# Two graph-attention layers on one core: edge places held as bytes, and layer 2 builds its edge masks instead of loading the stored ones

## The chip, the core and the metric

The kernel runs on one core of a Trainium2 chip. The metric is the device time of one launch in microseconds (us). The engines are PE (TensorE; its weight loads are listed apart as PEld), DVE (VectorE), ACT (ScalarE), POOL (GpSimd) and SP (SyncE), which only issues transfers here. [...]

## What is computed

The input is 6250 nodes with 768 numbers each and 100,000 directed edges, sorted by the node they end at. Each node is also given an edge to itself. Cut to what matters, the reference is:

```python
h = maximum(layernorm(x), 0)
for W, a_src, a_dst, heads in layers:        # 4 heads, then 1; 256 features
    h = h @ W
    e = leaky_relu(alpha_s[src] + alpha_d[dst], 0.2)    # alpha = sums of h * a
    alpha = softmax of e over the edges with the same dst
    h = relu(segment_sum(h[src] * alpha, dst) + bias)
out = x + (relu(h @ Wm1 + bm1) @ Wm2 + bm2)
```

Every edge needs a row of its source node (a gather), a number of its target node (found through a mask), and has to be added up at its target node (a product with a one-hot matrix).

## The kernel before, in words

**Phase 1** (lines 301 to 459) normalises x, multiplies it by W1 and stores 49 blocks of 128 rows as `table[1]`. Beside it a generator, `edge_places` (line 189), turns the target indices into places within a block of 128. It makes two forms. `dcol` (line 126) has one place per edge for each lane, in f32. `dmod_d` (line 127) is a DRAM copy of all places in a row, in bf16; they are made in `drm` (line 206) and stored at line 214. Padding edges have a bit far above 127 set, so that they match no lane.

**Layers.** `layer_edges` (line 525) is run for layer 1 and for layer 2. The edges are cut into tiles of 128 edges, four tiles are a group g, and four groups are a block t of 128 target nodes. There are NG = 196 groups and NT = 49 blocks, so 782 real tiles per layer. The loop at line 705 goes over g, with j = g % 4:

- `gather(g + 8)` (line 551, POOL) fetches the rows of four tiles, eight groups ahead. There are ten buffers G.
- `pair(g, 0)` and `pair(g, 1)` (line 611) each treat two tiles: two exponentials on ACT (lines 619, 621), short products on DVE (lines 624, 627 or 634), then the weighted operand `hw` on DVE (line 636 in layer 1, two instructions at line 631 in layer 2), then two products on PE (line 647) that add up in `o_ps`.
- `make_hot(g + 1)` (line 581, DVE) builds the one-hot operand, in layer 1 only.
- at j = 0: `fetch_rows(t + 4)` (line 513), which loads the places of 16 tiles, spread to all 128 lanes, into a `drow` buffer (three of them, shared with other uses), again in layer 1 only; `node.prefetch(t)`, which in layer 2 loads x; and `meet(t + 1)` (line 591), 16 small bf16 products of the masks with a table `win`, which give each edge its target's number.
- at j = 1 and j = 3: `make_mask((g + 7) // 2)`.
- `gather_up(g - 2)` (line 658): DVE adds `o_ps` of two groups back into a running sum (`acc`, line 672), and ACT copies a quarter of it (line 680).
- `advance(g)` steps the work of finished blocks: `Node1.steps` (line 794) or `Node2.steps` (line 900), with transposes and products on PE, copies on ACT (`rT`, line 767) and, in layer 2, the output store on SP (line 946).

A mask covers eight tiles: 128 lanes by 1024 edges in bf16, one where the edge's place equals the lane. This is the function around the change:

```python
            def make_mask(u):
...
                if layer == 2:
                    return fetch_mask(u + 1)
                a, b = (t * P for t in both(u))
                mask[u] = maskp.tile([P, 8 * P], BF16, name="mask")
...
                nc.vector.tensor_scalar(mask[u][:, a:b], drow[u // 2][:, at + a:at + b], pidx, None,
                                        ALU.is_equal)
                nc.sync.dma_start(mask_d[u * P:(u + 1) * P], mask[u])
```

So layer 1 makes each of its 98 masks on DVE (line 570) and stores it to DRAM (`mask_d`, line 299, stored at 572). Layer 2 loads the same masks back (line 523). Both layers use the same six mask buffers in turn. Five loads are issued at the end of layer 1 (line 753).

**The order of the work is written out by hand** (`manual_schedule`, line 300): each engine gets its instructions in the order of the Python program, and waits are put in where data or buffers demand them. SP's queue holds, in that order, the loads of places, masks and x, and the stores of masks, table rows and outputs; a store that waits for its data holds up what stands behind it.

Between the layers, `first_rows`, `first_hits` and `first_whole` (lines 288, 249, 262) let the first tiles of a layer start before the last blocks of its table are stored. `first_hits` compares source indices, as 32-bit integers kept in a `drow` buffer, with node numbers (line 258, DVE). `hold` (line 848) checks the limits of the method in block 3 of layer 2 and uses three `drow` buffers for it. If its flag is set, `general` runs at the end; with these inputs it isn't.

Of the kernel before, what the change touches and what calls it, by code (L numbers as in the profile page):

```python
# [10 lines left out]
F32 = mybir.dt.float32  # L11
BF16 = mybir.dt.bfloat16
I32 = mybir.dt.int32
AF = mybir.ActivationFunctionType
ALU = mybir.AluOpType
AX = mybir.AxisListType

P = 128
# [15 lines left out]
NET = NG * TPG  # L34
FIRST = LEAD // P
LAST = -(-(LEAD + E) // P)
NU = NG // 2
# [5 lines left out]
CH = P * TPC  # L43
NCH = EP // CH
# [9 lines left out]
def kernel(  # L54
# [21 lines left out]
    nc = tc.nc  # L76
# [7 lines left out]
    dram = pool("dram", 1, space=bass.MemoryType.DRAM)  # L84
# [38 lines left out]

    src_i = const.tile([P, NET], I32, name="src_i")
    dst_f = const.tile([P, NET], F32, name="dst_f")
    dcol = const.tile([P, NET], F32, name="dcol")
    dmod_d = dram.tile([NCH, CH], BF16, name="dmod_d")
    flags = const.tile([P, 4], F32, name="flags")


# [58 lines left out]
    def edge_places(ones):  # L189

        dst_i = ones.tile([P, NET], I32, name="dst_i")
        dri = ones.tile([NCH, CH], I32, name="dri")
        for to, of in ((dst_i, dst_cols), (dri, dst_rows), (src_i, src_cols)):
            nc.sync.dma_start(to, of)
            yield
            yield
        for layer in bT:
            with nc.allow_non_contiguous_dma(reason="256 numbers"):
                nc.sync.dma_start(bT[layer], {1: b1, 2: b2}[layer].rearrange("(k p) -> p k", p=P))
            yield  # L200
        b = ones.tile([P, OUT_DIM // P], F32, name="b")
        with nc.allow_non_contiguous_dma(reason="768 numbers"):
            nc.sync.dma_start(b, bm2.rearrange("(p k) -> p k", p=P))
        yield

        drm = ones.tile([NCH, CH], BF16, name="drm")
        nc.scalar.activation(dst_f, dst_i, AF.Copy)
        yield
        for d, to in ((dst_i, dcol), (dri, drm)):
            nc.vector.tensor_scalar(d, d, PAD_DST | P - 1, None, ALU.bitwise_and)  # L210
            yield
            nc.scalar.activation(to, d, AF.Copy)
            yield
        nc.sync.dma_start(dmod_d, drm)
        bp = ones.tile([P, 3, OUT_DIM // P], BF16, name="bp")
        rest = ones.tile([P, 2, OUT_DIM // P], F32, name="brest")
        in_parts(nc.vector, [bp[:, k] for k in range(3)], b, rest[:, 0], rest[:, 1])
        yield
        with nc.allow_non_contiguous_dma(reason="768 numbers"):
            nc.sync.dma_start(bm2_d.rearrange("s (p k) -> p s k", p=P), bp)  # L220
# [5 lines left out]
    rowsp = edges_stack.enter_context(tc.tile_pool(name="rows", bufs=3))  # L226
    maskp = edges_stack.enter_context(tc.tile_pool(name="masks", bufs=6))
# [11 lines left out]
    def first_sources(layer):  # L239

        n = len(THERE[layer])
        sources[layer] = []
        for j in range(0, n, 8):
            m = min(n - j, 8)
            of = rowsp.tile([P, 16 * P], BF16, name="drow").bitcast(I32)
            nc.sync.dma_start(of[:, :m * P], bcast(src_rows, m * P, (FIRST + j) * P))
            sources[layer].append(of)

# [39 lines left out]
    def first_rows(layer, stage):  # L288
# [3 lines left out]
        for j in range(j, j + n):  # L292
            g, t = divmod(FIRST + j, TPG)
            if g not in first_G[layer]:
# [1 line left out]
            nc.gpsimd.indirect_dma_start(  # L296
                out=first_G[layer][g][:, t], out_offset=None, in_=table[layer][:there * P],
                in_offset=bass.IndirectOffsetOnAxis(ap=first_i[layer][:, j:j + 1], axis=0))
    mask_d = dram.tile([NU * P, 8 * P], BF16, name="mask_d")
    edges_stack.enter_context(tc.manual_schedule())  # L300
    with tc.tile_pool(name="w1p", bufs=1) as wp, tc.tile_pool(name="x1", bufs=6) as xp, \
            tc.tile_pool(name="wk1", bufs=3) as wk, tc.tile_pool(name="once", bufs=1) as ones:
# [200 lines left out]
    drow, mask = {}, {}  # L503
# [9 lines left out]
    def fetch_rows(r):  # L513

        if r < NET // 16:
            drow[r] = rowsp.tile([P, 16 * P], BF16, name="drow")
            nc.sync.dma_start(drow[r], bcast(dmod_d, 16 * P, r * 16 * P))

    def fetch_mask(u):

        if u < NU:
            mask[u] = maskp.tile([P, 8 * P], BF16, name="mask")
            nc.sync.dma_start(mask[u], mask_d[u * P:(u + 1) * P])

    def layer_edges(layer, H, node, pre, matched, pre_pool):

# [3 lines left out]
        with tc.tile_pool(name=f"eg{layer}", bufs=4) as eg, \  # L530
# [28 lines left out]
            def make_mask(u):  # L559

                if not 0 <= u < NU:
                    return
                if layer == 2:
                    return fetch_mask(u + 1)
                a, b = (t * P for t in both(u))
                mask[u] = maskp.tile([P, 8 * P], BF16, name="mask")
                if u == 0:
                    nc.vector.memset(mask[u][:, :a], 0.0)
                at = u % 2 * 8 * P
                nc.vector.tensor_scalar(mask[u][:, a:b], drow[u // 2][:, at + a:at + b], pidx, None,  # L570
                                        ALU.is_equal)
                nc.sync.dma_start(mask_d[u * P:(u + 1) * P], mask[u])

            def make_hot(g):

# [108 lines left out]
            def advance(g):  # L684

                for _ in range(2 if NG - 4 <= g < NG - 2 else 1):
                    for step in list(late):
                        if next(step, 0) == 0:
                            late.remove(step)

            if layer == 1:
                for r in range(4):
                    fetch_rows(r)
                first_whole(pre_pool, layer)
                for u in range(4):
                    make_mask(u)
            make_hot(0)
            for g in range(AHEAD):
                gather(g)
# [5 lines left out]
            for g in range(NG):  # L705
                t, j = divmod(g, 4)
                if g == NG - 2:
                    at_end.append(g)
                gather(g + AHEAD)
                pair(g, 0)  # L710
                if g == NG - 1:
                    pair(g, 1)
                if g >= NG - 2:
                    gather_up(g - 1)
                advance(g)
                if g <= NG - 4:
                    make_hot(g + 1)
                if g in (NG - 4, NG - 3):
                    make_hot(g + 2)
                if j == 0:  # L720
                    if layer == 1:
                        fetch_rows(t + 4)
                    node.prefetch(t)
                    meet(t + 1)
                elif j == (2 if t < NT - 1 else 1):
                    node.ahead(t)
                elif j % 2:
                    make_mask((g + 7) // 2)
                if g == NG - 3:
                    idle_ps.append(ps.tile([P, 4 * P], F32, name="idle_ps", tag="e"))  # L730
                if g >= NG - 3:
                    stay_warm(3)
                if g < NG - 1:
                    pair(g, 1)
                advance(g)
                if j == 3:
                    join(t + 1)
                if g < NG - 2:
                    gather_up(g - 2)
                if g == NG - 3:  # L740
                    gather_up(g - 1)
                if NG - 3 <= g < NG - 1:
                    stay_warm(3)
                G.pop(g)
                hot.pop(g, None)
                if layer == 1 and g == NG - 6:
                    first_sources(2)
# [1 line left out]
            advance(NG)  # L749
            stay_warm(4)  # L750
            if layer == 1:
                for k in range(5):
                    fetch_mask(k)
            while late:
                advance(NG)
            at_end.clear()
# [70 lines left out]
    with tc.tile_pool(name="wmp", bufs=1) as wp, tc.tile_pool(name="x3", bufs=4) as xp, \  # L827
# [7 lines left out]
        pre2 = SimpleNamespace()  # L835
        bad_i = const.tile([1, 1], I32, name="bad_i")

# [9 lines left out]

        def hold(ok):
            bad = ok.tile([P, 4], F32, name="bad")
            rel = rowsp.tile([P, 16 * P], BF16, name="drow").bitcast(F32)[:, :NET]  # L850
            nc.vector.tensor_sub(rel, dst_f, wbase.rearrange("p g t -> p (g t)"))
            nc.vector.tensor_reduce(flags[:, 2:3], rel, AX.X, ALU.min)
            far = rowsp.tile([P, 16 * P], BF16, name="drow").bitcast(F32)[:, :NET]
            nc.vector.tensor_scalar(far, dst_f, float(N), -float(PAD_DST), ALU.is_ge, ALU.mult)
            rel2 = rowsp.tile([P, 16 * P], BF16, name="drow").bitcast(F32)[:, :NET]
            nc.vector.tensor_add(rel2, rel, far)
            nc.vector.tensor_reduce(flags[:, 3:4], rel2, AX.X, ALU.max)
            nc.vector.tensor_scalar(bad[:, 0:2], flags[:, 0:2], LIMIT, None, ALU.is_gt)
            nc.vector.tensor_scalar(bad[:, 2:3], flags[:, 2:3], 0.0, None, ALU.is_lt)
            nc.vector.tensor_scalar(bad[:, 3:4], flags[:, 3:4], float(P), None, ALU.is_ge)  # L860
            n_ps = ps.tile([1, 4], F32, name="n_ps", tag="n")
            nc.tensor.matmul(n_ps, ones_c, bad, start=True, stop=True)
            n_sb = ok.tile([1, 1], F32, name="n_sb")
            nc.vector.tensor_reduce(n_sb, n_ps, AX.X, ALU.add)
            nc.vector.tensor_scalar(bad_i, n_sb, 1.0, None, ALU.min)
# [387 lines left out]
```

## Time and profile before

| | us |
|---|---|
| median of 3 runs | 2591.09 (2585.95 to 2595.64) |
| the profiled execution | 2642.57 |
| its span, first to last instruction | 2640.8 |
| phase 1, up to the last mask before loop 1 | about 0 to 205 |
| loop of layer 1, first to last `acc` | 214.8 to 1427.5 |
| loop of layer 2, first to last `acc` | 1483.9 to 2621.8 |

| engine | busy us | share of the span |
|---|---|---|
| PE | 1657.0 | 63% |
| DVE | 1415.1 | 54% |
| ACT | 560.3 | 21% |
| POOL | 1598.5 | 61% |

The profile is one execution and is about 2% longer than the median; shares and durations are read from it. "Idle before, releaser" says how long an engine stood still ahead of an instruction and which other one let it go; "issue" means that the profile shows nothing that it waited for. Four groups of transfers concern the change: `drow<-dmod_d` (49 of 512 KB), `mask_d<-mask` (98 of 256 KB), `mask<-mask_d` (98 of 256 KB) and, for size, everything together, 383.24 MB.

### The profile page before, as it was taken

How to read it: one execution, taken by the hardware profiler on the slowest of the kernel's cores; microseconds unless marked ns; L12 is line 12 of the kernel's file. 1: busy time of each engine (PE TensorE's matmuls, PEld its weight loads, DVE VectorE, ACT ScalarE, POOL GpSimd, SP SyncE). 2: the span in 40 equal slices, each digit the busy share in tenths (PEclk: the TensorE clock that was granted, in tenths of full speed). 3: DMA queues.
4: the chain of work that ended last, by engine and by line, in shares of the span. 5: the costliest groups of instructions: out<-in, count | busy, mean ns of one | idle time of the engine just before them, and what ended most of it. 6: DMA issues, size and time to landing. Idle time of an engine off the chain costs nothing. (4 is left out here: it accounts for less than half of the span.)

```text
span 2640.8 us, 26321 instructions
## 1 busy us (share of the span) xinstructions
PE 1657.0 (63%) x6763; PEld 1115.4 (42%) x6765; DVE 1415.1 (54%) x4359; ACT 560.3 (21%) x2601; POOL 1598.5 (61%) x1759
## 2 busy tenths in 40 slices
PE   9955556554655555555457366766666676676676
PEld 7843333333433333333335244444444444444454
DVE  7935556555655555555556354444445444444454
ACT  5521111111111111111112122222222222222122
POOL 7865666655665556556653666666666666666661
PEclk9977766777677677777778677787787778787878
DMA  9944445444444444444443444454444444454442
GB/s 358 339 144 145 136 126 145 124 136 122 134 138 127 133 130 138 129 129 136 130 117 105 132 128 130 146 151 146 139 140 150 146 138 142 146 151 144 131 150 75
DMA packets 157541, 383.24 MB, mean 145 GB/s; under 512 B 35543, under 2 KB 49966, under 8 KB 157382
## 3 DMA queue, kind: packets, MB, share of 16 engines
q0 software_dynamic: 75072, 209.10, 29.2%
q1 hardware_dynamic: 80940, 170.88, 19.2%
q10 hardware_dynamic: 1370, 1.48, 0.2%
q8 instruction: 58, 0.95, 0.1%
q14 instruction: 101, 0.83, 0.1%
HBM read 323.13 MB, written 58.19 MB: 144 GB/s over the span
## 5 line engine op out<-in xcount | busy, mean ns | idle before, releaser
L551 POOL DMA_INDIRECT G<-table,src_i x1545 | 1467.8, 950 | 908.1 <-issue 747.6
L647 PE MATMUL o_ps<-hw,hot 128*128 128x260 f32 x1564 | 604.3, 520 | 532.7 <-DVE hw L636 216.3
L647 PEld LDWEIGHTS o_ps<-hw,hot 128*128 128x128 f32 x1564 | 353.9, 248 | 750.2 <-DVE hw L636 301.4
L647 PE MATMUL o_ps<-G,hw 128*128 128x258 f32 x1564 | 500.2, 455 | 208.3 <-issue 107.6
L647 PEld LDWEIGHTS o_ps<-G,hw 128*128 128x128 f32 x1564 | 337.0, 227 | 342.8 <-issue 156.7
L680 ACT ACTIVATE sum<-acc 32x260 f32<-32x260 f32 (+1 forms) x384 | 159.9, 416 | 1489.1 <-DVE acc L672 829.4
L624 DVE TENSOR_TENSOR e_ps<-e,e_ps 128x8 f32<-128x8 f32 (+1 forms) x782 | 127.7, 163 | 561.5 <-ACT e L621 359.5
L672 DVE SCALAR_TENSOR_TENSOR acc<-acc,keep,o_ps 128x260 f32<-128x260 f32 (+1 forms) x388 | 185.3, 478 | 220.4 <-remote 203.7
L631 DVE TENSOR_SCALAR hw<-iota_ps,dcol,w 128x128 f32<-128x128 f32 x782 | 285.0, 406 | 31.4 <-DVE w L627 17.5
L636 DVE TENSOR_TENSOR hw<-G,e_ps 128x520 f32<-128x520 f32 x391 | 271.9, 695 | 48.3 <-DVE e_ps L634 29.8
L937 PE MATMUL y_ps<-wm,mT 128*128 128x384 f32 x392 | 197.2, 621 | 105.0 <-issue 60.6
L619 ACT ACTIVATE e<-G 128x8 f32<-128x8 f32 (+1 forms) x782 | 155.4, 199 | 95.0 <-issue 30.2
L937 PEld LDWEIGHTS y_ps<-wm,mT 128*128 128x128 f32 x392 | 82.4, 231 | 182.1 <-issue 119.8
L621 ACT ACTIVATE e<-G 128x8 f32<-128x8 f32 (+1 forms) x782 | 150.2, 192 | 0.0
L940 DVE TENSOR_TENSOR y<-y_ps,xt 128x384 f32<-128x384 f32 (+1 forms) x98 | 54.2, 553 | 175.5 <-remote 127.7
L346 PE MATMUL h_ps<-w,r 128*128 128x256 f32 x588 | 133.0, 380 | 4.3 <-ACT r L337 4.3
L581 DVE TENSOR_TENSOR hot<-iota_ps,dcol 128x512 f32<-128x512 f32 (+1 forms) x196 | 133.6, 682 | 0.0
L346 PEld LDWEIGHTS h_ps<-w,r 128*128 128x128 f32 x588 | 108.0, 190 | 21.7 <-ACT r L337 5.5
L767 ACT ACTIVATE rT<-tp,bT 128x128 f32<-128x128 f32 x196 | 60.2, 357 | 217.7 <-remote 175.8
L634 DVE TENSOR_TENSOR e_ps<-e_ps,e 128x8 f32<-128x8 f32 x391 | 68.1, 174 | 54.9 <-remote 29.8
L921 PE MATMUL tp<-rT,wm 128*128 128x128 f32 x392 | 64.9, 318 | 29.0 <-ACT rT L767 27.8
L921 PEld LDWEIGHTS tp<-rT,wm 128*128 128x128 f32 x392 | 61.9, 230 | 40.3 <-ACT rT L767 35.3
(405 smaller groups left out, 1175.0 us busy)
## 6 DMA issues: line engine op xcount, KB each, us to landing
xt<-in_x SPq DMA_DIRECT2D x96, 384.0 KB
drow<-dmod_d SPq DMA_DIRECT2D x49, 512.0 KB
mask_d<-mask SPq DMA_DIRECT2D x98, 256.0 KB
mask<-mask_d SPq DMA_DIRECT2D x98, 256.0 KB
G<-table,src_i POOLq DMA_INDIRECT x1545
xTt<-in_xT SPq DMA_DIRECT2D x49, 384.0 KB
out<-y SPq DMA_DIRECT2D x48, 384.0 KB
table<-kept SPq DMA_DIRECT2D x49, 132.0 KB
```

The lines of the kernel that those rows point to most:

```text
L346: nc.tensor.matmul(h_ps, r[:, k], w1[:, k], start=(k == 0), stop=(k == KI - 1))
L551: nc.gpsimd.indirect_dma_start(out=G[g][:, t], out_offset=None, in_=table[layer], in_offset=bass.IndirectOffsetOnAxis(ap=src_i[:, k:k + 1] ...
L581: nc.vector.tensor_tensor(hot[g][:, T[0]:T[0] + n], iota_ps.unsqueeze(1).to_broadcast([P, n, P]), dcol[:, k:k + n].unsqueeze(2).to_broadca ...
L619: nc.scalar.activation(e1, sc, AF.Exp)
L621: nc.scalar.activation(e2, sc, AF.Exp, scale=SLOPE)
L624: nc.vector.tensor_mul(v, e2, rho)
L631: nc.vector.tensor_scalar(hw[:, t], iota_ps, dcol[:, k:k + 1], w[:, t], ALU.is_equal, ALU.mult)
L636: nc.vector.tensor_mul(hw, Gp[:, :, :RW[1]].rearrange("p t (h c) -> p t h c", h=H), w.unsqueeze(3).to_broadcast([P, 2, H, C + 1]))
L647: nc.tensor.matmul(o_ps[g], l, r[:, :RW[layer]], start=(k == tiles(g)[0]), stop=(k == TPG - 1))
L672: nc.vector.scalar_tensor_tensor(acc, run[0], keep[:, k:k + 1], o_ps.pop(g), ALU.mult, ALU.add)
L680: nc.scalar.activation(done[t][r], acc[r], AF.Copy)
L937: nc.tensor.matmul(y_ps, mT[:, j], wm2[:, j, s * half:(s + 1) * half], start=False, stop=(j == KH - 1))
```

## The change

The places are stored as unsigned bytes. Padding edges, which don't fit in a byte, are cut to 255, which matches no lane either. The `drow` buffers and `dmod_d` take half of their former bytes. Layer 2 no longer loads masks: it fetches the places (`fetch_rows`) and makes its masks from them with the same DVE instruction and at the same points of the loop as layer 1. `mask_d`, its stores and its loads are gone. The 32-bit uses of the old `drow` buffers get two buffers of their own (`of`). In `edge_places` one ACT copy becomes a DVE instruction. The core of the diff:

```diff
-    dmod_d = dram.tile([NCH, CH], BF16, name="dmod_d")
+    dmod_d = dram.tile([NCH, CH], U8, name="dmod_d")
...
-        for d, to in ((dst_i, dcol), (dri, drm)):
+        for d in (dst_i, dri):
             nc.vector.tensor_scalar(d, d, PAD_DST | P - 1, None, ALU.bitwise_and)
             yield
-            nc.scalar.activation(to, d, AF.Copy)
-            yield
+        nc.scalar.activation(dcol, dst_i, AF.Copy)
+        yield
+        nc.vector.tensor_scalar(drm, dri, 255.0, None, ALU.min)
+        yield
...
-            of = rowsp.tile([P, 16 * P], BF16, name="drow").bitcast(I32)
+            of = rowsp.tile([P, 8 * P], I32, name="of", bufs=2)
...
-            drow[r] = rowsp.tile([P, 16 * P], BF16, name="drow")
+            drow[r] = rowsp.tile([P, 16 * P], U8, name="drow")
             nc.sync.dma_start(drow[r], bcast(dmod_d, 16 * P, r * 16 * P))
-
-    def fetch_mask(u):
-
-        if u < NU:
-            mask[u] = maskp.tile([P, 8 * P], BF16, name="mask")
-            nc.sync.dma_start(mask[u], mask_d[u * P:(u + 1) * P])
...
-                if layer == 2:
-                    return fetch_mask(u + 1)
                 a, b = (t * P for t in both(u))
                 mask[u] = maskp.tile([P, 8 * P], BF16, name="mask")
...
                 nc.vector.tensor_scalar(mask[u][:, a:b], drow[u // 2][:, at + a:at + b], pidx, None,
                                         ALU.is_equal)
-                nc.sync.dma_start(mask_d[u * P:(u + 1) * P], mask[u])
...
+            for r in range(4) if layer == 1 else (3,):
+                fetch_rows(r)
             if layer == 1:
-                for r in range(4):
-                    fetch_rows(r)
                 first_whole(pre_pool, layer)
-                for u in range(4):
-                    make_mask(u)
+            for u in range(4):
+                make_mask(u)
...
                 if j == 0:
-                    if layer == 1:
-                        fetch_rows(t + 4)
+                    fetch_rows(t + 4)
...
             if layer == 1:
-                for k in range(5):
-                    fetch_mask(k)
+                for r in range(3):
+                    fetch_rows(r)
```

## The prediction

> **What bounds the kernel now.** I read the page first, then the list of waits, then the timeline of single blocks. The page shows no full engine: PE is busy 63% of the span, DVE 54%, POOL 61%, at a PE clock that changes between whole and half.
>
> ```profile
> PE 1657.0 (63%) x6763; PEld 1115.4 (42%) x6765; DVE 1415.1 (54%) x4359; ACT 560.3 (21%) x2601; POOL 1598.5 (61%) x1759
> PEclk9977766777677677777778677787787778787878
> ```
>
> The list of waits seems to name POOL, the gathers, and then a ring of DVE, ACT and PE.
>
> ```profile
> ACT sum L680 <- DVE acc L672: 829.4, 185, 18.0
> POOL G L551 <- issue: 747.6, 1415, 13.3
> DVE e_ps L624 <- ACT e L621: 359.5, 217, 13.5
> PEld o_ps L647 <- DVE hw L636: 301.4, 155, 13.0
> ```
>
> POOL is not the bound. I paired the gathers, in order, with the exponentials that read them (line 619): from the end of a gather's issue to its first reader it takes 43 to 68 us in layer 1 and 32 to 49 us in layer 2. POOL runs eight groups ahead and stands still because its ten buffers are full. What remains is the ring. In a clean stretch of layer 1 the timeline (start, duration, engine) shows it:
>
> ```profile
> 699.42 0.68 DVE L581 TENSOR_TENSOR hot<-iota_ps,dcol 128x512 f32<-128x512 f32 x1
> 700.02 0.48 DVE L570 TENSOR_SCALAR mask<-drow,pidx 128x1024 bf16<-128x1024 bf16 x1
> 700.41 0.17 DVE L624 TENSOR_TENSOR e_ps<-e,e_ps 128x8 f32<-128x8 f32 x1
> ...
> 701.70 0.48 DVE L672 SCALAR_TENSOR_TENSOR acc<-acc,keep,o_ps 128x260 f32<-128x260 f32 x1
> 702.21 0.42 ACT L680 ACTIVATE sum<-acc 32x260 f32<-32x260 f32 x1 [3.65 <-DVE acc L672]
> ...
> 702.98 0.17 DVE L624 TENSOR_TENSOR e_ps<-e,e_ps 128x8 f32<-128x8 f32 x1 [0.81 <-ACT sum L680]
> ```
>
> DVE has no gap around the mask: the next instruction starts 0.39 us after it. DVE stands still only 0.81 us per group, while ACT copies `acc` and then makes the next exponentials behind it in its queue. So DVE's work and that turn through ACT add up to the period. Measured from one `acc` to the next over the whole trace, DVE stands still under 1.2 us in 71% of layer 1's groups (0.93 on average over these) and in 59% of layer 2's (0.91). There, an instruction added to DVE is paid in full.
>
> In the other groups PE holds up the ring. Layer 2 at 2018 us:
>
> ```profile
> 2018.84 0.19 PEld L647 LDWEIGHTS o_ps<-G,hw 128*128 128x128 f32 x1 [0.51 <-issue]
> 2020.25 0.38 PE L647 MATMUL o_ps<-G,hw 128*128 128x258 f32 x1 [1.51 <-DVE hw L631]
> 2020.96 0.19 PEld L647 LDWEIGHTS o_ps<-G,hw 128*128 128x128 f32 x1 [1.94 <-issue]
> ...
> 2028.94 0.62 ACT L767 ACTIVATE rT<-tp,bT 128x128 f32<-128x128 f32 x2 [10.61 <-remote]
> ...
> 2029.78 0.17 DVE L624 TENSOR_TENSOR e_ps<-e,e_ps 128x2 f32<-128x2 f32 x1 [10.29 <-ACT e L621]
> ```
>
> For 11 us PE starts something only every 0.7 us or a multiple of it, with nothing that it waits for, and DVE stands still 10.29 us. I counted 99 such stretches in the two layers (at most five PE starts within 2.8 us, for over 2 us), 726 us in all. What causes them the trace doesn't say. In layer 2 they mostly lie some 130 PE instructions apart, which the change leaves as they are, so I take their number and length as given.
>
> [...] 1024 bf16 elements and 512 four-byte ones (line 258) both take 0.39 us from start to start. [...] No row of this trace has a byte operand. [...] the 81 gathers that overlap a mask in layer 1 take 0.950 us, the others 0.953; and POOL has over 30 us in hand. [...] The trace has half clock in 676 us of loop 1 and 502 us of loop 2[...].
>
> **The change, part by part.** The price of a byte mask is the open term. The rows:
>
> ```profile
> L581 DVE TENSOR_TENSOR hot<-iota_ps,dcol 128x512 f32<-128x512 f32 x195 | 133.2, 683 | 0.0
> L570 DVE TENSOR_SCALAR mask<-drow,pidx 128x1024 bf16<-128x1024 bf16 x97 | 48.5, 502 | 0.0
> ...
> L258 DVE TENSOR_SCALAR hit<-drow,nid 128x512 f32<-128x512 int32 x8 | 3.4, 486 | 0.0
> ```
>
> Durations overlap by some 0.08 us, so I use start to start: mask 0.39, `hit` of 512 elements 0.39, `hot` of 512 elements 0.60[...]. Upper bound[...]: `tensor_reduce` takes 552 ns for 392 elements (line 499) and 971 for 784 (line 852), 1.07 ns each, so 0.60 + 512 x 1.07 = 1.15 us. Middle[...]: `hit` of 768 elements takes 605 ns, of 256 351, 0.5 ns each, so 0.39 + 512 x 0.5 = 0.65 us. Lower bound, as bf16: 0.39. I take 0.65[...].
>
> *Layer 1's masks get slower:* 98 x (0.65 - 0.39) = 25.5 us of DVE. After 21 of the 94 masks in the loop a DVE gap of over 1.5 us begins within 2.6 us, a wait for PE that swallows the delay. That leaves 78%: 20 us.
>
> *Layer 2's masks are new on DVE:* 94 x 0.65 = 61 us in the loop. I looked at the places where they come, between the two pairs of odd groups: a gap follows within 2.6 us at 33 of 98 and within 4 us at 47. I let 40% be swallowed: 37 us. At j = 3 nearly nothing is: that period is 3.47 us at the median and still at the third quartile. Queued behind a mask on DVE are `pair(g, 1)` and `acc`; for `acc` waits ACT, and for both PE's products. The four masks ahead of the loop (2.5 us) stand before `prepare` in DVE's order, where DVE idles 1.0 us at 1433 and 1.1 us at 1438 now: 1.5 us left.
>
> *New waits:* a mask of layer 2 waits for its `drow`. It is fetched two blocks (some 47 us) ahead, and its buffer was read a block before, so SP isn't held by it; output stores ahead of it in SP's queue (longest wait 48.7 us) can eat that lead, not more than once. Lower bound 0, upper 5 us; I take 0. Layer 1's `fetch_rows` keeps its place.
>
> *Gone:* 98 stores (25.7 MB) and 98 loads of masks, half of layer 1's places; layer 2 gets 12.8 MB of places. Nobody waits for the stores; the mask matmuls of line 599 lost 10.7 us to "issue" in all and none to the loads. Value 0; had these transfers slowed PE, the gain is the last rival's. SP's mask issues end with them: SP is waited for by nobody here.
>
> *Phase 1:* one DVE instruction of some 1.1 us (line 210's size) for an ACT one, 196 KB stored as 98, beside a PE that is 94% busy: 0.
>
> Sum: 20 + 37 + 1.5 = 58.5 us on the profiled 2642.57, so 2701. The median stands at 0.981 of that execution: 58.5 x 0.981 = 57, **2591 + 57 = 2648 us**, 2.2% slower. Without swallowing, 25.5 + 63.5 = 89 us, 2678; with two thirds swallowed, 30 us, 2620; at the lower price of 0.39, layer 1 pays nothing and layer 2 94 x 0.39 x 0.6 = 22 us, 2613.
>
> **The rivals.**
> *A, forecast:* 2648, chance 0.50.
> *B[...]:* 98 x 0.76 x 0.78 = 58, 94 x 1.15 x 0.6 = 65, 3.5 at the start: 127 us, 2715; 187 us and 2774 if nothing is swallowed. For it: no byte operand is seen[...]. [...] Chance 0.23.
> *C, PE swallows more:* each mask delays a ring that PE's pauses reset anyway; a third is paid, 30 us, 2620. For it: layer 2's PE is busy 68% of the window 1600 to 2200. Against it: the clean groups above. Chance 0.15.
> *D, faster: PE's pauses are an effect of the transfers.* Layer 1 loses 38.5 of its some 160 MB (24%), layer 2 12.8 of some 170 (7.5%). Did the pauses (about 350 and 375 us) shrink alike, that is 84 + 28 = 112 us, less 58.5: 2539. It decides from pauses shorter by 8%. Against it: in the pauses DMA is quieter, not busier:
>
> ```profile
> 2018.90:2028.90 10.00, 2.72 (x6) 1.28 (x6) 0.59 (x2) 0.00 (x0) 5.36 (x6) 0.73 0.35 93
> 2030.00:2042.00 12.00, 11.02 (x55) 7.81 (x55) 8.54 (x31) 3.61 (x18) 9.07 (x10) 0.84 0.67 210
> ```
>
> The last two numbers are DMA's share and GB/s; phase 1 has 323 GB/s and no such pause. Chance 0.10. The rest, 0.02, is no difference at all.
>
> **How the numbers follow.** The likeliest is A, 2648; alone it spans 2620 to 2678. The range of 8 in 10 leaves out D and the end of B: 2607 to 2730. About 0.5% (13 us) is what a measurement tells from no change. Faster by more is D but for a bit, 0.09; within it the low end of C and the rest, 0.06; slower 0.85.
>
> **What would show it.** Right: line 570 has 196 entries, start to start 0.65 us; layer 2's period at j = 3 grows from 3.47 to 4.1 us and layer 1's clean groups at j = 1 and 3 by 0.26; the count of pauses stays near 99. Wrong: a mask of 0.39 or 1.15 us; j = 3 unchanged; pauses fewer or shorter, or a new wait for `drow` in the list.

## The result and the profile after

| | us |
|---|---|
| kernel before, beside the changed one, median of 4 | 2588.52 (2577.85 to 2595.64) |
| changed kernel, median of 4 | 2615.94 (2612.40 to 2622.67) |
| ratio, 95% interval | 1.0112 (1.0069 to 1.0156) |
| profiled executions | 2642.57 before, 2612.44 after |

The change costs 27 us, 1.1%. Forecast were 57; the sign was right, the size twice too large. The two profiled executions can't simply be subtracted: that of before is 54 us above its median, that of after lies within 0.1 us of the lowest of its four. So I compare them by parts. The page's first part and its clock row:

```profile
PE 1676.4 (64%) x6764; PEld 1118.3 (43%) x6765; DVE 1503.1 (58%) x4459; ACT 560.9 (21%) x2600; POOL 1630.4 (62%) x1759
...
PEclk9976776877767677777778688878887787878878
```

DVE is busy 88.0 us longer than before (1415.1), which is the 89 us that the masks were to cost if nothing hid them. POOL is busy 31.9 us longer, though it executes the same instructions; this becomes important below. The list of waits:

```profile
ACT sum L673 <- DVE acc L665: 782.6, 199, 21.0
POOL G L547 <- issue: 665.5, 1359, 12.0
PEld o_ps L640 <- issue: 501.3, 462, 5.8
DVE e_ps L617 <- ACT e L614: 478.7, 255, 9.6
PE o_ps L640 <- issue: 349.3, 336, 5.4
```

The columns are total us, times, longest. No new wait for `drow` stands among the large ones. PE waits 850 us at the edge products for "issue", which is nothing that the profile shows; before, it was 590 us (343.6 and 246.5). So the pauses are still there. They are not PE's alone: ahead of `e_ps` DVE, too, waited for "issue" in both profiles. The rows of before, and then DVE's of after:

```profile
PEld o_ps L647 <- issue: 343.6, 303, 8.8
PE o_ps L647 <- issue: 246.5, 197, 8.4
DVE e_ps L624 <- issue: 84.8, 92, 6.8
```

```profile
DVE e_ps L617 <- issue: 50.8, 70, 1.1
```

The groups, shape by shape, with busy us and mean ns, give the price of a mask:

```profile
L564 DVE TENSOR_SCALAR mask<-drow,pidx 128x1024 bf16<-128x1024 uint8 x194 | 145.2, 750 | 0.0
...
L564 DVE TENSOR_SCALAR mask<-drow,pidx 128x768 bf16<-128x768 uint8 x2 | 1.1, 559 | 1.5 <-DMA drow<-dmod_d 1.5
```

Two records of layer 1, in the timeline of DVE, give it from start to start:

```profile
1012.70 0.68 DVE L574 TENSOR_TENSOR hot<-iota_ps,dcol 128x512 f32<-128x512 f32 x1
1013.30 0.77 DVE L564 TENSOR_SCALAR mask<-drow,pidx 128x1024 bf16<-128x1024 uint8 x1
1013.99 0.15 DVE L617 TENSOR_TENSOR e_ps<-e,e_ps 128x8 f32<-128x8 f32 x1
```

The mask takes 0.69 us here. In groups without a pause it is paid in full, as forecast: the median period in layer 1 goes from 4.21 to 4.47 us at j = 1 and from 4.61 to 4.86 at j = 3; in layer 2, j = 3, from 3.47 to 4.12. Yet the loops didn't grow. Each line is one loop (start and end, length, busy us of PE, PEld, DVE, ACT, POOL, then clock, DMA share, GB/s), first before, then after:

```profile
215.00:1428.00 1213.00, 680.24 (x2587) 434.82 (x2587) 690.17 (x1915) 212.82 (x1148) 705.05 (x741) 0.72 0.46 128
1484.00:2622.00 1138.00, 768.91 (x3236) 513.46 (x3235) 550.06 (x1977) 246.98 (x1194) 701.67 (x741) 0.78 0.47 140
```

```profile
217.00:1416.00 1199.00, 677.39 (x2586) 435.17 (x2587) 713.44 (x1917) 214.10 (x1148) 716.28 (x741) 0.74 0.39 99
1475.00:2593.00 1118.00, 781.16 (x3234) 511.89 (x3235) 610.27 (x2071) 247.04 (x1194) 720.32 (x740) 0.81 0.46 132
```

DVE works 23 us longer in layer 1 and 60 us longer in layer 2, and stands still so much less that both loops are shorter. In the two loops its gaps of over 2 us fall from 113 gaps with 666 us in all to 94 with 580 us; the stretches with few PE starts, by the count of the prediction, from 99 with 726 us to 87 with 625. The list of waits, which counts short waits for "issue" as well, had PE's grow. So the pauses are there in both profiles, but they are not the same pauses. In layer 2 most blocks now take 23.4 to 23.6 us, with one pause each; in the profile before the middle half took 21.4 to 25.3. One such pause of the changed kernel:

```profile
1860.94 0.38 PE L640 MATMUL o_ps<-G,hw 128*128 128x258 f32 x1 [0.24 <-issue]
...
1863.05 0.38 PE L640 MATMUL o_ps<-G,hw 128*128 128x258 f32 x1 [1.74 <-issue]
...
1868.91 0.62 ACT L759 ACTIVATE rT<-tp,bT 128x128 f32<-128x128 f32 x2 [7.52 <-remote]
...
1869.76 0.17 DVE L617 TENSOR_TENSOR e_ps<-e,e_ps 128x2 f32<-128x2 f32 x1 [7.20 <-ACT e L614]
```

The slots are still 0.7 us or a multiple, but DVE stands still 7.2 us here, for 10.29 in the pause that the prediction shows.

### The profile page after: what moved, and what is told of

It reads as the page before. It is cut to its first block, busy times and chain, and to the rows that moved or that the text cites. A ratio compares the mean times of both kernels' runs of the same rounds, so it can differ in the third digit from the quotient of the medians.

```text
span 2610.5 us, 26086 instructions
## 1 busy us (share of the span) xinstructions
PE 1676.4 (64%) x6764; PEld 1118.3 (43%) x6765; DVE 1503.1 (58%) x4459; ACT 560.9 (21%) x2600; POOL 1630.4 (62%) x1759
## 4 chain that ended last, share of the span: by engine, by line
DVE 32%; issue 22%; PE 19%; another core or an unknown queue 16%; ACT 6%; DMA 4%; POOL 1%; ACTq 0%; POOLq 0%; SPq 0%; DVEq 0%
PE o_ps L640 9%; DVE hw L629 8%; DVE hw L624 5%; PE h_ps L348 4%; DVE mask L564 4%; DMA G<-table,src_i 3%; DVE e_ps L617 3%; PE y_ps L928 3%; DVE acc L665 3%; ACT sum L673 2%; DVE e_ps L627 2%; ACT e L612 2%; PE tp L912 1%; DVE w L620 1%
## 5 line engine op out<-in xcount | busy, mean ns | idle before, releaser
L547 POOL DMA_INDIRECT G<-table,src_i x1545 | 1499.1, 970 | 851.5 <-issue 665.5
L640 PE MATMUL o_ps<-hw,hot 128*128 128x260 f32 x1564 | 591.5, 509 | 476.2 <-DVE hw L629 207.2
L640 PE MATMUL o_ps<-G,hw 128*128 128x258 f32 x1564 | 523.1, 457 | 250.7 <-issue 185.4
L640 PEld LDWEIGHTS o_ps<-G,hw 128*128 128x128 f32 x1564 | 328.3, 224 | 416.6 <-issue 288.3
L928 PE MATMUL y_ps<-wm,mT 128*128 128x384 f32 x392 | 174.6, 555 | 38.4 <-issue 37.5
L564 DVE TENSOR_SCALAR mask<-drow,pidx 128x1024 bf16<-128x1024 uint8 (+1 forms) x196 | 146.1, 748 | 1.5 <-DMA drow<-dmod_d 1.5
L928 PEld LDWEIGHTS y_ps<-wm,mT 128*128 128x128 f32 x392 | 72.2, 203 | 100.3 <-issue 77.1
L592 PE MATMUL e_ps<-win,mask 128*128 128x12 bf16 (+1 forms) x1564 | 61.1, 168 | 50.3 <-issue 43.2
L912 PE MATMUL tp<-rT,wm 128*128 128x128 f32 x392 | 79.0, 368 | 21.3 <-ACT rT L759 21.2
```

The lines of the kernel that those rows point to most:

```text
L547: nc.gpsimd.indirect_dma_start(out=G[g][:, t], out_offset=None, in_=table[layer], in_offset=bass.IndirectOffsetOnAxis(ap=src_i[:, k:k + 1] ...
L640: nc.tensor.matmul(o_ps[g], l, r[:, :RW[layer]], start=(k == tiles(g)[0]), stop=(k == TPG - 1))
L928: nc.tensor.matmul(y_ps, mT[:, j], wm2[:, j, s * half:(s + 1) * half], start=False, stop=(j == KH - 1))
```

## The experiments

The theory after the result, S: a pause of PE takes back most of the DVE time that is added near it. Its rival, T: DVE's time is paid as forecast, and some 30 us come back since 51 MB of mask transfers are gone. Each kernel was timed beside the kernel before, on the same chip.

**The kernel before again.**

> The kernel before once more, as a measure of the noise and for a second profile of it. Every theory: ratio 1.000, at most 0.3% off. The first profiled execution lay 2% above the median; if that excess sat in PE's pauses, this profile has fewer than 99 of them or shorter ones (726 us in the first).

Measured: 2135.95 us, ratio 1.0001 (0.9994 to 1.0008). The same kernel that took 2588 us in the first comparison takes 2136 us in this one, and 2136 to 2139 in all later ones, on four chips. Part of its page, and two of its waits:

```profile
PE 1599.9 (75%) x6763; PEld 1085.4 (51%) x6765; DVE 1414.6 (66%) x4359; ACT 592.9 (28%) x2601; POOL 1600.0 (75%) x1759
...
POOL 6877777777777777777777777777777777777774
```

```profile
ACT e L619 <- DMA G<-table,src_i: 561.8, 405, 5.3
...
PEld o_ps L647 <- issue: 9.6, 29, 1.5
```

PE's wait for "issue" at the edge products is 9.6 us, for 343.6 in the first profile: the long pauses don't come from the kernel alone. DVE's waits for "issue" are gone as well. Which chip the first comparison ran on isn't recorded, so the chip isn't excluded as their cause. Without them another bound appears. ACT's exponentials wait 561.8 us for gathered rows, and POOL's row has no dip. From the first gather of layer 1 (143.6 us) to the last of layer 2 (2109.8) POOL issues one gather after another, 0.95 us each and 0.30 to the next; all its longer gaps together are 2.0 us. Sixteen of them are 20.0 us, and that is the block. So in this setting the time is 144 us before the first gather, POOL's chain, and 24 us after it. The next kernels test what this setting pays for; what the first comparison paid for needs pauses, and comes after.

**Byte places in layer 1 alone** (the changed kernel, with `mask_d`, its stores and layer 2's loads as before):

> Byte places in layer 1 alone; its masks are stored and layer 2 loads them, as before. Theory S (PE's pauses take back most of DVE's added time): of 25.5 us of added DVE time about a third is paid, 2597 us (+8). Rival T (DVE's time is paid as forecast, and the absent transfers give some 30 us back): 20 us are paid, 2608 us. In both the groups at j = 1 and j = 3 of layer 1 that have no pause grow by 0.26 us.

Measured: 2152.60 us, 1.0080 (1.0066 to 1.0094), +16.4 us.

**bf16 places, layer 2 builds its masks, no mask transfers:**

```diff
-            drow[r] = rowsp.tile([P, 16 * P], U8, name="drow")
+            drow[u] = rowsp.tile([P, 8 * P], BF16, name="drow")
...
-                nc.vector.tensor_scalar(mask[u][:, a:b], drow[u // 2][:, at + a:at + b], pidx, None,
+                nc.vector.tensor_scalar(mask[u][:, a:b], drow[u][:, a:b], pidx, None,
```

> Places stay bf16 (halves of a block fetched one by one, so that they fit), layer 2 builds its masks, nothing is stored or loaded as masks. Layer 1's DVE time is that of before, layer 2 gets 94 x 0.39 = 37 us. Theory S: a third of it is paid, 2600 us (+12). Rival T: 60% of it is paid (22 us), and about half of the 30 us comes back, since half of the bytes are saved: 2595 us. If bytes cost what is forecast, this is 15 us or more below the changed kernel.

Measured: 2138.09 us, 1.0009 (1.0002 to 1.0016), +1.9 us: building layer 2's masks is nearly free here, so the bytes are what costs.

**The mask transfers put back:**

```diff
+                if layer == 1:
+                    nc.sync.dma_start(mask_d[u * P:(u + 1) * P], mask[u])
+                else:
+                    fetch_spare(u + 1)
```

> The changed kernel, with the mask stores of layer 1 put back and in layer 2 a load of a stored mask into a spare buffer that nobody reads: DVE, PE and ACT have the work of the changed kernel, SP and the DMA engines nearly that of the kernel before. Theory S: as the changed kernel, 2616 us (+27). Rival T: the 30 us are lost again, 2646 us (+57).

Measured: 2178.45 us, 1.0204 (1.0190 to 1.0218), +42.3 us.

**The changed kernel again, and two that make its masks dearer.** By now gathers beside a byte mask had been seen to take longer, hence theory L.

> The changed kernel once more, beside the other two, since the kernel before took 2136 us in the last four runs and 2588 us beside the changed kernel. Theory L (where PE's pauses are short POOL sets the pace, 16 gathers of 1.25 us or 20.0 us a block, and a byte mask lengthens the gather that it overlaps, 1.06 to 1.11 us for 0.955): some 0.3 us more per block in both layers, 1.3% slower (ratio 1.013). Rival D (DVE's own time is paid, 30% of 89 us): also about 1.012. If PE's pauses are long again: 1.011 as in the first comparison.

Measured: 2168.28 us, 1.0146 (1.0129 to 1.0162), +31.5 us. The timeline of POOL and of the masks in it:

```profile
1708.61 0.95 POOL L547 DMA_INDIRECT G<-table,src_i  x1 [0.30 <-issue]
...
1709.51 0.74 DVE L564 TENSOR_SCALAR mask<-drow,pidx 128x1024 bf16<-128x1024 uint8 x1
...
1709.86 1.21 POOL L547 DMA_INDIRECT G<-table,src_i  x1 [0.30 <-issue]
...
1718.63 0.74 DVE L564 TENSOR_SCALAR mask<-drow,pidx 128x1024 bf16<-128x1024 uint8 x1
...
1718.87 1.32 POOL L547 DMA_INDIRECT G<-table,src_i  x1 [0.30 <-issue]
```

The masks end at 1710.25 and 1719.37, the gathers that began in them at 1711.07 and 1720.19: 0.82 us later both times. Of all 155 gathers that begin during a mask, the 5th to the 95th percentile end 0.81 to 0.82 us after it. The gather doesn't run slower; it stands still until the mask has ended. A gather that is already under way can be stopped too, as the one at 300.00 is:

```profile
300.00 1.07 POOL L547 DMA_INDIRECT G<-table,src_i  x1 [0.30 <-issue]
300.20 0.74 DVE L564 TENSOR_SCALAR mask<-drow,pidx 128x1024 bf16<-128x1024 uint8 x1
```

All 24 gathers that begin 0.15 to 0.45 us ahead of a mask end some 0.12 us after it; none of the 100 that begin 0.62 us or more ahead is held. So the mask stops a gather of 0.95 us at two places: about 0.13 us after its start and about 0.12 us before its end.

The first of the two dearer kernels makes the mask with another instruction:


```diff
-                nc.vector.tensor_scalar(mask[u][:, a:b], drow[u // 2][:, at + a:at + b], pidx, None,
-                                        ALU.is_equal)
+                nc.vector.tensor_tensor(mask[u][:, a:b], drow[u // 2][:, at + a:at + b],
+                                        pidx.to_broadcast([P, b - a]), ALU.is_equal)
```

> The changed kernel with the mask made by tensor_tensor from the same bytes[...]: about 1.1 us for 0.65, so some 85 us more DVE time in all. Theory L: if this form doesn't lengthen the gathers beside it, they return to 0.95 us and the time falls to within 0.5% of before (ratio 1.000 to 1.005), though DVE works longer. Rival D: 30% of 85 us on top, ratio 1.023 or more.

Measured: 2232.76 us, 1.0455 (1.0437 to 1.0473), +96.0 us. That form doesn't spare the gathers: those that overlap a mask take 1.18 us. So holding gathers up isn't peculiar to tensor_scalar; this instruction is longer (1215 ns a record for 761) and holds them up longer. But it holds them at the first place only. Of the 194 gathers that begin in such a mask 148 are stopped, and of the 23 that begin 0.15 to 0.45 us ahead of one, none:

```profile
1709.48 0.94 POOL L547 DMA_INDIRECT G<-table,src_i  x1 [0.30 <-issue]
1709.65 1.22 DVE L564 TENSOR_TENSOR mask<-drow,pidx 128x1024 bf16<-128x1024 uint8 x1
```

The kernel with each mask of layer 2 made twice:

> The changed kernel with each mask of layer 2 made twice, 98 x 0.65 = 64 us more DVE time in layer 2. Theory L: another 0.3 us per block of longer gathers in layer 2, 15 us, ratio 1.020. Rival D: 30% of 64 us, ratio 1.021. If layer 2 has no room left on DVE: 64 us, ratio 1.04. With long pauses of PE, theory S: about a third or less of 64 us in layer 2.

Measured: 2183.94 us, 1.0220 (1.0205 to 1.0235), +47.2 us, which both theories allow.

**Where the lane numbers lie.** The tensor_tensor form reads two inputs from SBUF, the places and the lane numbers. The next kernel takes one of them from PSUM:

```diff
-    iota_ps = ps.tile([P, P], F32, name="iota_ps", bufs=1)
+    iota_ps = ps.tile([P, P + 1], F32, name="iota_ps", bufs=1)
+    pidx_ps = iota_ps[:, P:]
...
+                nc.vector.tensor_tensor(mask[u][:, a:b], drow[u // 2][:, at + a:at + b],
+                                        pidx_ps.to_broadcast([P, b - a]), ALU.is_equal)
```

> The mask again by tensor_tensor[...], but with the lane numbers read from PSUM instead of SBUF: the same 85 us of added DVE time as the tensor_tensor form before it, one SBUF source instead of two. Theory P (two SBUF operands of a DVE instruction hold up the gather beside it): gathers beside a mask take 0.95 to 0.96 us, POOL's chain is as long as before, ratio 1.000 to 1.004. Rival Y (bytes, or the length of the instruction, hold up the gather): as the other tensor_tensor form, gathers 1.18 us, ratio 1.045. Rival D (DVE's own time): 1.023 or more.

Measured: 2138.56 us, 0.9999 (0.9991 to 1.0007). The same DVE work as the form before it, and 94 us less. Its timeline, POOL and masks:

```profile
1708.87 1.21 DVE L567 TENSOR_TENSOR mask<-drow,iota_ps 128x1024 bf16<-128x1024 uint8 x1
...
1709.40 0.94 POOL L550 DMA_INDIRECT G<-table,src_i  x1 [0.30 <-issue]
```

No gather beside a mask takes longer than 0.96 us. With tensor_scalar's own number read from PSUM nothing changes against the changed kernel (ratios 1.0147 and 1.0146). So that number isn't the input that matters, and what in tensor_scalar holds the gathers up was not shown:

> The changed kernel's tensor_scalar with its one number per lane read from PSUM. If that number counts as an operand in theory P[...], gathers go back to 0.95 us and the ratio to 1.000 to 1.004; if it is read once and doesn't matter, as the changed kernel: gathers 1.055 us, ratio 1.0146.

Measured: 2171.05 us, 1.0147 (1.0131 to 1.0164).

Put together, in us against the kernel before of the same comparison; gathers and DVE are the busy times of the pages, against 1469.1 and 1414.6 in the repeat of before. The rows of the gathers, repeat of before and changed kernel:

```profile
L551 POOL DMA_INDIRECT G<-table,src_i x1545 | 1469.1, 951 | 471.8 <-issue 357.8
L547 POOL DMA_INDIRECT G<-table,src_i x1545 | 1502.4, 972 | 471.5 <-issue 359.4
```


| kernel | time | gathers | DVE |
|---|---|---|---|
| bytes in layer 1 alone | +16.4 | +16.5 | +25 |
| bf16, built in layer 2 | +1.9 | +4.8 | +43 |
| changed kernel | +31.5 | +33.3 | +92 |
| changed, transfers put back | +42.3 | +43.8 | +87 |
| changed, layer 2's masks twice | +47.2 | +49.3 | +166 |
| tensor_tensor, SBUF | +96.0 | +87.5 | +180 |
| tensor_tensor, PSUM | 0.0 | -0.9 | +179 |
| tensor_scalar, number in PSUM | +32.4 | +32.9 | +93 |

The time follows the gathers, line by line, within 3 us (8.5 in the dearest form), and not DVE. With the transfers put back it follows them too: gathers take 979 ns for 972. Why they do, I did not test.

**Pauses made on purpose.** To price the change where POOL has room, both kernels got pauses of PE at every fifth group:

```diff
+                    if g % 5 == 2 and k == 0:
+                        for _ in range(32):
+                            nc.tensor.matmul(o_ps[g], l, r[:, :RW[layer]], start=True, stop=True)
```

> The kernel before with PE pauses made on purpose: in every fifth group the first product is issued 32 more times (each overwrites the last, the result stays). That is some 8 to 13 us of PE per pause, 78 pauses, so that blocks take some 25 us, over POOL's 20.0, as in the profile of the 2591 us execution. Expected 2136 + 78 x (7 to 10) less what POOL's pace had hidden: 2400 to 2650 us. It is the base for the next run; POOL should stand still for its buffers again.

> The changed kernel with the same pauses. Against the kernel before with pauses: forecast (22% and 40% of the added DVE time swallowed): +57 us. Nothing swallowed: +89 us. Theory S (a pause takes back most of what stands near it): +27 us or less. Theory L (POOL's longer gathers are all that costs): about 0 here, since POOL has room.

Measured: 2508.23 us (1.1719, 1.1703 to 1.1735) and 2548.25 us (1.1895, 1.1879 to 1.1912): the change costs 40.0 us, more than S said and less than the forecast. The two loops, before and after with pauses, columns as above:

```profile
188.00:1308.00 1120.00, 1018.70 (x5076) 840.78 (x5076) 690.10 (x1916) 215.07 (x1148) 715.38 (x752) 0.97 0.49 140
1334.00:2484.00 1150.00, 1130.00 (x5726) 905.68 (x5725) 546.81 (x1977) 246.57 (x1196) 721.31 (x760) 1.00 0.47 141
```

```profile
194.00:1324.00 1130.00, 1025.57 (x5069) 842.41 (x5069) 712.39 (x1916) 215.09 (x1148) 726.95 (x751) 0.97 0.41 107
1356.00:2537.00 1181.00, 1138.84 (x5724) 902.79 (x5724) 607.63 (x2071) 246.18 (x1194) 736.15 (x754) 1.00 0.44 127
```

Of the added DVE time layer 1 pays 10 of 22 us and layer 2 31 of 61, half in all. Another 12 us lie outside the loops: the first starts 6 us later, and the stretch between them grows from 26 to 32 us. These two executions lie 52 us apart where the medians lie 40, so half is the upper end. POOL's gathers are 34.1 us longer here too, and POOL has room for it: beyond the 0.30 us between gathers it stands still 325 us in the one and 340 in the other.

> The changed kernel with the made pauses and with the mask transfers put back as in the run with spare traffic (stores in layer 1, loads into a spare buffer in layer 2). DVE's and PE's work is that of the changed kernel with pauses (2548 us, 1.1895 of before). Theory H (the pauses alone take DVE's time back, the transfers are worth nothing): the same time within 0.4%. Rival D (the absent transfers give some of it back): 10 to 30 us more, 2558 to 2578 us, 1.194 to 1.204.

Measured: 2548.03 us, 1.1929 (1.1912 to 1.1946): the time of the changed kernel with pauses to 0.2 us, by the ratios 7 us more. The transfers are worth 0 to 7 us there, less than the 10 to 30 of the rival.

> The form with bf16 places, layer 2 building its masks, with the made pauses: 37 us of DVE time more than the kernel before. Theory H with a paid share of 0.45: 17 us over the kernel before with pauses, 2525 us, 1.180 of before. Nothing paid: 2508 us, 1.172; all paid: 2545 us, 1.189.

Measured: 2529.83 us, 1.1847 (1.1832 to 1.1863), 22 us over the kernel before with pauses, by the ratios 27: more than the 17 expected. The loops pay 10 us of 37 by the profile, and the stretch between them 9.5, which a share of DVE's time left out. The 10 are 17 more in layer 2 and 6.5 less in layer 1, where DVE's work is that of before. The rows of the gathers, kernel before with pauses and this one, are alike:

```profile
L551 POOL DMA_INDIRECT G<-table,src_i x1545 | 1469.4, 951 | 744.8 <-issue 587.5
L547 POOL DMA_INDIRECT G<-table,src_i x1545 | 1469.4, 951 | 766.8 <-issue 587.1
```

So what is paid here isn't the gathers; in the setting without pauses the same form cost 1.9 us.

> The PSUM tensor_tensor form of the mask, which cost nothing where POOL sets the pace, with the made pauses. It has 88 us more DVE time than the changed kernel. Theory H with a paid share of 0.45: 40 us over the changed kernel with pauses, 2588 us, 1.208 of before. If DVE has room in the pauses for all of it: 2548 us. If no room is left: 88 us more, 2636 us, 1.233.

Measured: 2626.26 us in the middle of six runs; the ratio, 1.2209 (1.2152 to 1.2267), is that of the three shortest. The size stays uncertain: the six go from 2585.81 to 2636.26 us as PE's clock goes from 0.982 to 0.960. The one run at the clock of the other pause kernels took 2585.81, 38 us over the changed kernel with pauses, near the 40 expected, but one run settles nothing. What is seen is that the form that costs nothing where POOL sets the pace isn't free where it doesn't: every one of the six is over the longest run of the changed kernel with pauses (2556.83).

## Why the prediction was half right

**The price of a byte mask** held: 0.69 us at the place shown for 0.65, 750 ns a record, DVE 88.0 us longer for a sum of 89. The 0.65 was the author's estimate from the 0.5 ns an element of the four-byte comparison. Rival B, with 1.15 us, is out.

**"There, an instruction added to DVE is paid in full"** held for groups without a pause: +0.26 and +0.25 us in layer 1, +0.65 in layer 2.

**The shares failed.** "That leaves 78%: 20 us" and "I let 40% be swallowed: 37 us" are the terms that were mis-sized, and with them the forecast. They came from asking whether a gap of DVE begins within a few microseconds of a mask. With made pauses half of it is paid in the loops, 41 us of 83 in the profiles, where the forecast had 57 of 86.5. In the first comparison it is less: 27 us in all, though DVE's work in the loops grows by 83. A reason that fits, but that no run shows by itself: a pause doesn't have to follow a mask closely, since a ring that is late at a pause has less to wait for in it, wherever the delay arose before. Rival C, which said so and gave 30 us, was the nearest; its share, a third, isn't the half of the made pauses, so that it came so near is partly luck. What part of the fall in DVE's long gaps, 666 to 580 us, comes from this, what from the unequal executions and what from the absent transfers (rival D in part), stays open. DVE's own waits for "issue", for one, are 34 us less in the profile after (84.8 and 50.8), which no term of the prediction has. The long pauses didn't come back in any later run, and what makes them isn't known. With made pauses a share is taken back, and there the transfers count for little.

**"POOL is not the bound"** was true of the profiled execution and of nothing after it. Where PE's pauses are short, POOL sets the pace, and the reading that a gather takes as long beside a mask (0.950 us) as elsewhere (0.953) failed with it. The mean over 81 gathers hid it: only 10 of them began in a mask, and 3 of these were held up (1.03 to 1.11 us). The change makes masks of 0.65 us for 0.39, and twice as many. There the change costs 31.5 us, and its 92 us of DVE time cost nothing. That this is near the 27 us of the first comparison is a coincidence of two causes: there POOL stood still 851.5 us ahead of its gathers, for 471.5 where it sets the pace, and had room.

**"1.5 us left" at the boundary and 0 for phase 1** came out at about 6 us each with made pauses. For the boundary the reading was wrong: the four masks stand ahead of the whole preparation of layer 2 in DVE's order, the first waits 0.95 us for its places, and the gaps that were to hide them come later. How much of the first 6 us is the change's stays open: the kernel with the transfers put back has the same phase 1, and its loop starts 1.3 us later than that of before.

**"Gone: value 0"** held within 7 us with pauses. Where POOL sets the pace the transfers are worth some 11 us (ratios 1.0204 and 1.0146).

**PE's clock** was not lower with the longer DVE path: in the two loops the granted clock was 0.74 and 0.81, for 0.72 and 0.78 before.

No kernel beat the one before; where POOL sets the pace, the PSUM form equals it without mask transfers.

## What to carry to other kernels

Before a wait is called harmless, ask how much of the profile's setting it rests on: POOL's pace, 20.0 us a block where blocks took some 24 to 26, was the bound as soon as the pauses were short. A cost on an engine is to be asked for in what else it holds: here 92 us of DVE time cost nothing and the 0.17 us by which each mask held a gather up (33.3 us over 196 masks) cost 31. Where a loop has pauses, measure the paid share of added work with pauses made on purpose, and don't read it from how near a gap lies; even then the pauses made may not be the ones that were met.

## What was unexpected of the hardware

A gather's issue on POOL that began while DVE made a byte mask ended 0.82 us after the mask, so it was stopped and not slowed; one that began 0.15 to 0.45 us ahead of it ended 0.12 us after it. The `tensor_tensor` mask of 1.22 us with both inputs in SBUF stopped 148 of the 194 gathers that began in it and none of the 23 that began 0.15 to 0.45 us ahead of it; those that overlapped it took 1.18 us. With one input in PSUM, at 1.21 us, it stopped none (0.96 us at most). Why the two forms differ in what they stop was not shown.

The bf16 mask of before, at 0.39 us from start to start, stopped gathers as well, but it is short: in the repeat of before 43 gathers began in one, and the 25 that began 0.12 to 0.30 us into it were held up and ended 0.81 to 0.82 us after it.

And one program, unchanged, took 2588 us in one comparison and 2136 to 2139 in four others. The first had long pauses, in which PE's slots are 0.7 us apart and DVE, too, waits for nothing that the profile shows. What makes them the traces don't say.
